# Adding up a selective scan's outputs with fp32 transposes in PSUM instead of identity products

## The chip, the cores and the metric

The kernel runs on one core of a Trainium2 chip. The metric is device time in microseconds (us) of one execution of the whole program. The engines are named as in the profile: PE (TensorE, matrix products; PEld are its weight loads), DVE (VectorE), ACT (ScalarE), POOL (GpSimd) and SP, which issues the DMA transfers.

## The reference, cut to what matters

The network has four layers on an image batch of shape 4 x 64 x 64 x 96. Layers 0 and 1 are state-space blocks ("block 0" and "block 1" here); layers 2 and 3 are attention and feed-forward layers on the pixels. Nearly all of the time goes to the two state-space blocks. Each of them scans its feature map in four directions: along rows, along columns, and both of these backwards. Block 1 works on the 64 x 33 half spectrum of the image.

```python
def step(hst, inputs):                       # one position l
    ul, dl, bl, cl = inputs
    dA = jnp.exp(dl[..., None] * A)          # A: channels x 16 states
    hst = hst * dA + (dl * ul)[..., None] * bl[:, :, None, :]
    y = jnp.einsum('bkdn,bkn->bkd', hst, cl) # sum over the 16 states of h * C
    return (hst, y)
...
ys = ys + Dskip[None, :, :, None] * u
...                                          # _cross_merge: the four directions joined
ys = ys[:, 0:2] + ys[:, 2:4][..., ::-1]
y1 = jnp.swapaxes(ys[:, 1].reshape(b, d, w, h), 2, 3).reshape(b, d, h * w)
y = ys[:, 0] + y1
...
y = (y - mu) * jax.lax.rsqrt(var + LN_EPS) * out_norm_w + out_norm_b
y = y * jax.nn.silu(z)
return y @ out_proj_w.T
```

What matters below is the sum over the 16 states of `h * C`, and how the four directions' sums meet: two of them are in row order and two in column order.

## The kernel before

Channels lie on the 128 partitions in three groups (`c`), positions along the free dimension. A direction is cut into segments of at most 512 positions. For a segment the 16 states are done in four quarters `q` of four states; one step of the loop does one quarter of one channel group: states 4q and 4q+1 as `hx`, 4q+2 and 4q+3 as `hy`. Per step DVE runs four hardware scans along the positions, POOL makes `hcx = hx * C` and the input of `hy`, DVE makes `hcy = hy * C`, ACT makes the exponentials and the scaled inputs `bx`, and PE transposes `bx` and adds up `hcx` and `hcy` in a PSUM bank for each channel group.

Six phases follow one another: two of block 0 (two images at a time, 384 steps each) and four of block 1 (one image each, 240 steps). Beside each phase a generator of "side" work is run in small pieces, at a fixed rate per step: the projections and convolutions of what comes next, and the merge, norm, output projection and later layers of what is done. `RATES` has the pieces per step.

```python
RATES = [0.65, 1.2, 2.0, 1.85, 1.85, 1.75]
CFG0 = Cfg("l0", 2, 1, HH, 0, 6, [(0, 32), (32, 64)], [8] * 8, [512] * 8, 1e-5)
CFG1 = Cfg("l1", 1, 2, WF, 1, 12, [(0, WF)], [7, 7, 7, 6, 6], [448, 448, 448, 384, 384], 1e-5)
# the last lists: rows of a norm block, positions of a segment

def accumulate(st, hc, n0):                  # L549: sum over states
    z = st.z
    for j in range(2):
        nc.tensor.matmul(z.acc[st.c][:, : z.S], ident, hc[:, j, : z.S],
                         start=(n0 + j == 0 and not z.opened), stop=(n0 + j == NST - 1))

def open_segment(z, before):                 # cut
    ...
    z.opened = z.k != 1
    for c in range(C):
        if z.k == 0:                         # L569: the skip term, once for all directions
            nc.tensor.matmul(z.acc[c][:, : z.S], z.blk.skip[:, c, :], z.u[:, c, : z.S], start=True, stop=False)
        if z.k >= 2:                         # L573: go on from the forward direction's sum
            yv = sp.tile([P, SM], F32, name=f"yv_{z.nm}_{c}", tag="yv", bufs=2)
            nc.sync.dma_start(out=yv[:, : z.S], in_=z.ph.io["y"][z.k % 2][:, c, z.a : z.a + z.S])
            nc.tensor.matmul(z.acc[c][:, : z.S], ident, yv[:, : z.S], start=True, stop=False)

# the loop over steps, cut (hx, hy, hcx and hcy each have one buffer)
    scan(st, hx, 0, st.ax[:, 0], st.px[0], 4 * q)          # DVE
    front_y(st, 1)                                         # ACT exp
    scan(st, hx, 1, st.ax[:, 1], st.px[1], 4 * q + 1)      # DVE
    ...
    nxt.px, nxt.ay = [transposed(nxt, 0)], {}              # PE, L501: 128x128 transposes of bx
    front_x(nxt)                                           # ACT exp
    nc.gpsimd.tensor_tensor(hcx[:, :, :S], hx[:, :, :S], z.c[q][0][:, :, :S], ALU.mult)
    take(bgen, per - per // 2); slot(False)                # ACT bx; side work
    scan(st, st.hy, 0, ...)
    nxt.px.append(transposed(nxt, 1))
    scan(st, st.hy, 1, ...)
    ...
    accumulate(st, hcx, 4 * q)                             # PE
    slot(True)                                             # side work
    nc.vector.tensor_tensor(hcy[:, :, :S], st.hy[:, :, :S], z.c[q][1][:, :, :S], ALU.mult)
    front_b(nxt)                                           # POOL: du * B into hy of the next step
    accumulate(st, hcy, 4 * q + 2)                         # PE
    if q == NQ - 1:                                        # the segment's sum leaves PSUM
        nc.scalar.copy(y[:, :S], z.acc[c][:, :S])          # ACT, L650
        nc.sync.dma_start(out=z.ph.io["y"][z.k % 2][:, c, z.a : z.a + S], in_=y[:, :S])

# side work: merge, cut. The two orders meet; `yo` is read with swapped axes
    pm = E.psum(f"py_{nm}_{r}")
    nc.tensor.matmul(pm[:, : n * 64], self.ident, v, start=True, stop=False)            # L283
    nc.tensor.matmul(pm[:, : n * 64].rearrange("p (r w) -> p r w", w=64), self.ident,   # L284
                     yo[:, :, r - p0 : r - p0 + n].rearrange("p w r -> p r w"), start=False, stop=True)
    E.defer(lambda v=v, pm=pm, n=n: nc.scalar.copy(v, pm[:, : n * 64]))
    ...                                                    # then to DRAM as `ym`; gated() reads `ym` and `gz`
```

Of the kernel before, what the change touches and what calls it, by code (L numbers as in the profile page):

```python
# [6 lines left out]
F32 = mybir.dt.float32  # L7
# [10 lines left out]
NB, HH, WW, CH = 4, 64, 64, 96  # L18
LTOK = HH * WW
WF = WW // 2 + 1  # L20
NST = 16
C, P = 3, 128
SM = 512
LATE = "late"

RATES = [0.65, 1.2, 2.0, 1.85, 1.85, 1.75]
# [22 lines left out]
CFG1 = Cfg("l1", 1, 2, WF, 1, 12, [(0, WF)], [7, 7, 7, 6, 6], [448, 448, 448, 384, 384], 1e-5)  # L49
# [44 lines left out]
class Block:  # L94
# [165 lines left out]
    def merge(self, E, g, ys, out):  # L260

        nc, cfg = self.nc, self.cfg
        ym = self.dram_tile("ym", (P, C, cfg.L), g)
        out["ym"] = ym
        PR = max(b - a for a, b in cfg.parts)
        with E.pool(f"{cfg.pre}mg{g}") as sp:
            for c in range(C):
                for p0, p1 in cfg.parts:
                    nm, pr = f"{cfg.pre}_{g}_{c}_{p0}", p1 - p0
                    yn = sp.tile([P, PR * 64], F32, name=f"yn_{nm}", tag="yn", bufs=2)  # L270
                    nc.sync.dma_start(out=yn[:, : pr * 64], in_=ys[cfg.nat][:, c, p0 * 64 : p1 * 64])
                    yo = sp.tile([P, 64, PR], F32, name=f"yo_{nm}", tag="yo", bufs=2)
                    nc.sync.dma_start(
                        out=yo[:, :, :pr],
                        in_=ys[1 - cfg.nat][:, c, :].rearrange("p (w r) -> p w r", r=cfg.NR)[:, :, p0:p1],
                    )
                    yield
                    for r, n in cfg.rows:
                        if not p0 <= r < p1:
                            continue  # L280
                        pm = E.psum(f"py_{nm}_{r}")
                        v = yn[:, (r - p0) * 64 : (r - p0 + n) * 64]
                        nc.tensor.matmul(pm[:, : n * 64], self.ident, v, start=True, stop=False)  # L283
                        nc.tensor.matmul(  # L284
                            pm[:, : n * 64].rearrange("p (r w) -> p r w", w=64),
                            self.ident,
                            yo[:, :, r - p0 : r - p0 + n].rearrange("p w r -> p r w"),
                            start=False,
                            stop=True,
                        )  # L290
                        E.defer(lambda v=v, pm=pm, n=n: nc.scalar.copy(v, pm[:, : n * 64]))
                        yield
                    nc.sync.dma_start(out=ym[:, c, p0 * 64 : p1 * 64], in_=yn[:, : pr * 64])
            yield

    def gated(self, E, g, ym, gz, out_proj):


        nc, cfg = self.nc, self.cfg
        with E.pool(f"{cfg.pre}nm{g}") as sp:  # L300
# [3 lines left out]
            def load(r, n):  # L304
                y = sp.tile([P, C, 512], F32, name=f"yb_{cfg.pre}_{g}_{r}", tag="yb", bufs=2)
                z = sp.tile([P, C, 512], F32, name=f"zb_{cfg.pre}_{g}_{r}", tag="zb", bufs=2)
                nc.sync.dma_start(out=y[:, :, : n * 64], in_=ym[:, :, r * 64 : (r + n) * 64])
                nc.sync.dma_start(out=z[:, :, : n * 64], in_=gz[:, :, r * 64 : (r + n) * 64])
                return y, z

            nxt = load(*cfg.rows[0])
            yield
            for b, (r, nr) in enumerate(cfg.rows):
                n = nr * 64
                nm = f"{cfg.pre}_{g}_{r}"
                y, z = nxt
                nxt = load(*cfg.rows[b + 1]) if b + 1 < len(cfg.rows) else None
# [62 lines left out]
def scans(tc, ctx, phases, ident):  # L380

# [164 lines left out]
    def accumulate(st, hc, n0):  # L546
        z = st.z
        for j in range(2):
            nc.tensor.matmul(  # L549
                z.acc[st.c][:, : z.S],  # L550
                ident,
                hc[:, j, : z.S],
                start=(n0 + j == 0 and not z.opened),
                stop=(n0 + j == NST - 1),
            )

    def open_segment(z, before):

        if z.first:
            z.state = [  # L560
                sp.tile([P, NST], F32, name=f"state_{z.nm}_{c}", tag=f"state{c}", bufs=2) for c in range(C)
            ]
        else:
            z.state = before.state
        z.acc = [ps.tile([P, 512], F32, name=f"acc_{z.nm}_{c}", tag=f"acc{c}") for c in range(C)]
        z.opened = z.k != 1
        for c in range(C):
            if z.k == 0:
                nc.tensor.matmul(z.acc[c][:, : z.S], z.blk.skip[:, c, :], z.u[:, c, : z.S], start=True, stop=False)  # L569
            if z.k >= 2:  # L570
                yv = sp.tile([P, SM], F32, name=f"yv_{z.nm}_{c}", tag="yv", bufs=2)
                nc.sync.dma_start(out=yv[:, : z.S], in_=z.ph.io["y"][z.k % 2][:, c, z.a : z.a + z.S])
                nc.tensor.matmul(z.acc[c][:, : z.S], ident, yv[:, : z.S], start=True, stop=False)  # L573
# [629 lines left out]
```

## Time and profile before

| | before |
|---|---|
| time, median of 3 runs | 14555.34 us (14533.06 to 14558.75) |
| span of the profiled execution | 14556.2 us |
| instructions | 140535 |
| mean granted PE clock | 0.919 |
| DMA | 1195619 packets, 1488.38 MB, mean 102 GB/s |
| POOL, products `du*B` and `hx*C` (L524, L630) | 3699.9 and 3716.2 us busy |
| DVE, product `hcy` (L644) | 1993.5 us busy |

The page gives each engine's busy time over the span. A group's line has the source line, engine, operation and tiles (`out<-in`), the shapes, the count, then the busy time and the mean duration of one, then the idle time of the engine just before such instructions and what ended it. A line of waits has who waited for whom, the total, how often, and the longest. In a timeline the first two numbers are start and duration. PE's matmuls overlap, so a group's busy time is less than count times mean. Where no row of the profile has a number asked for (the distance between two starts, the steps of a phase), it is counted from the starts and ends of the instructions in the same trace, and from its record of the granted clock.

### The profile page before, as it was taken

What the parts mean: (1) busy time and instruction counts of PE and PEld (TensorE: products, weight loads), DVE (VectorE), ACT (ScalarE), POOL (GpSimd) and SP (SyncE); (2) the same over time, 40 slices, a digit from 0 to 9 for tenths busy, and PEclk for the clock granted to TensorE, in tenths of its full rate; (3) what the DMA queues carried; (4) which work ended last, traced back from release to release, by engine and by line L of the source; (5) the groups of instructions that cost most, each with busy time, mean ns of one, the idle gap of its engine ahead of it and who ended that gap; (6) DMA issues with size and microseconds to landing.
All of it is one profiled execution on the core that took longest, in us unless ns stands there. A gap on an engine that the chain in (4) does not pass through costs nothing. (4 is left out here: it accounts for less than half of the span.)

```text
span 14556.2 us, 140535 instructions
## 1 busy us (share of the span) xinstructions
PE 12208.7 (84%) x42312; PEld 6312.6 (43%) x42312; DVE 10543.2 (72%) x10170; ACT 9388.2 (64%) x20401; POOL 7523.1 (52%) x3644
## 2 busy tenths in 40 slices
PE   5788888888888889889898888887888878888876
PEld 1344344434444444434544444444444444444434
DVE  0598788777886777786655676788767887678753
ACT  1577777776766667775555665676656666567643
POOL 0466666655655555564444454455544555445530
PEclk8899999999999999999998999899998999989885
DMA  4344444445443344435333333222332223322221
GB/s 116 106 115 116 111 115 112 111 113 133 123 107 108 108 101 111 127 98 145 103 107 99 119 114 90 86 78 93 114 88 86 79 91 114 90 88 76 78 98 27
DMA packets 1195619, 1488.38 MB, mean 102 GB/s; under 512 B 587043, under 2 KB 977903, under 8 KB 1178471
## 3 DMA queue, kind: packets, MB, share of 16 engines
q1 hardware_dynamic: 1194855, 1479.39, 35.5%
q8 instruction: 333, 5.46, 0.2%
q14 instruction: 431, 3.53, 0.1%
HBM read 1217.05 MB, written 262.06 MB: 102 GB/s over the span
## 5 line engine op out<-in xcount | busy, mean ns | idle before, releaser
L524 POOL TENSOR_TENSOR hy_l<-du_l,bc_l 128x1024 f32<-128x1024 f32 (+2 forms) x1728 | 3699.9, 2141 | 4770.6 <-DVE hcy_l L644 3063.7
L630 POOL TENSOR_TENSOR hcx_l<-hx_l,bc_l 128x1024 f32<-128x1024 f32 (+2 forms) x1728 | 3716.2, 2151 | 1271.0 <-PE acc_l L549 1074.3
L549 PE MATMUL acc_l<-hcy_l,ident 128*128 128x512 f32 (+2 forms) x6912 | 3177.1, 584 | 384.6 <-DVE hcy_l L644 381.9
L549 PE MATMUL acc_l<-hcx_l,ident 128*128 128x512 f32 (+2 forms) x6912 | 3326.6, 607 | 117.6 <-POOL hcx_l L630 114.4
L481 ACT ACTIVATE bx_l<-dut_l,bt_l 128x192 f32<-128x192 f32 (+2 forms) x6400 | 2847.5, 499 | 0.0
L644 DVE TENSOR_TENSOR hcy_l<-hy_l,bc_l 128x1024 f32<-128x1024 f32 (+2 forms) x1728 | 1993.5, 1154 | 596.7 <-PE acc_l L549 494.2
L506 ACT ACTIVATE ax_l<-delta_l,l_alog 128x512 f32<-128x512 f32 (+2 forms) x3456 | 2152.5, 670 | 75.2 <-DVE hx_l L529 75.1
L549 PEld LDWEIGHTS acc_l<-hcy_l,ident 128*128 128x128 f32 x6912 | 1315.2, 199 | 1949.6 <-issue 1048.5
L529 DVE TENSOR_TENSOR_SCAN hy_l<-ab_l,state_l,hy_l 128x448 f32<-128x448 f32 (+1 forms) x1512 | 1743.0, 1186 | 418.5 <-ACT ab_l L506 305.5
L529 DVE TENSOR_TENSOR_SCAN hx_l<-ax_l,state_l,ab_l 128x448 f32<-128x448 f32 (+1 forms) x1512 | 1735.8, 1182 | 327.7 <-PE ab_l L501 303.2
L529 DVE TENSOR_TENSOR_SCAN hy_l<-b_l,state_l,hy_l 128x512 f32<-128x512 f32 (+1 forms) x1368 | 1542.1, 1158 | 474.0 <-ACT b_l L506 370.5
L529 DVE TENSOR_TENSOR_SCAN hx_l<-ax_l,state_l,b_l 128x512 f32<-128x512 f32 (+1 forms) x1368 | 1538.0, 1155 | 320.9 <-PE b_l L501 290.9
L549 PEld LDWEIGHTS acc_l<-hcx_l,ident 128*128 128x128 f32 x6912 | 1275.4, 205 | 1011.7 <-issue 685.9
L506 ACT ACTIVATE ab_l<-delta_l,l_alog 128x448 f32<-128x448 f32 (+1 forms) x1824 | 1195.0, 655 | 708.6 <-DVE hx_l L529 677.2
L506 ACT ACTIVATE b_l<-delta_l,l_alog 128x512 f32<-128x512 f32 (+1 forms) x1632 | 1041.9, 638 | 721.7 <-DVE hx_l L529 665.2
L501 PE MATMUL ab_l<-ident,bx_l 128*128 128x128 f32 (+1 forms) x7296 | 1298.4, 288 | 218.1 <-DVE hy_l L529 123.0
L501 PEld LDWEIGHTS ab_l<-ident,bx_l 128*128 128x128 f32 (+1 forms) x7296 | 918.7, 145 | 1251.9 <-issue 633.3
L501 PE MATMUL b_l<-ident,bx_l 128*128 128x128 f32 x5760 | 988.3, 294 | 209.2 <-DVE hy_l L529 116.8
L650 ACT COPY y_l<-acc_l 128x512 f32<-128x512 f32 (+2 forms) x432 | 234.7, 543 | 1421.7 <-PE acc_l L549 1417.2
L501 PEld LDWEIGHTS b_l<-ident,bx_l 128*128 128x128 f32 x5760 | 728.1, 149 | 942.8 <-issue 375.2
L223 PE MATMUL pc_l<-pad_l,l_dg 128*128 128x512 f32 (+2 forms) x1944 | 854.4, 583 | 72.7 <-ACT uh_l L212 58.2
L542 ACT COPY state_l<-hx_l 128x2 f32<-128x2 f32 x1440 | 271.5, 189 | 540.5 <-DVE hx_l L529 538.3
(173 smaller groups left out, 10872.3 us busy)
## 6 DMA issues: line engine op xcount, KB each, us to landing
bc_l<-l_xd_l SPq DMA_DIRECT2D x1536, 256.0 KB
bc_l<-l_xd_l SPq DMA_DIRECT2D x576, 448.0 KB
bc_l<-l_xd_l SPq DMA_DIRECT2D x384, 384.0 KB
us_l<-l_u SPq DMA_DIRECT2D x64, 768.0 KB
l_y<-y_l SPq DMA_DIRECT2D x192, 256.0 KB
us_l<-l_u SPq DMA_DIRECT2D x48, 672.0 KB
l_y<-y_l SPq DMA_DIRECT2D x144, 224.0 KB
yv_l<-l_y SPq DMA_DIRECT2D x96, 256.0 KB
```

The lines of the kernel that those rows point to most:

```text
L223: nc.tensor.matmul(pc[:, : n * 64].rearrange("p (r w) -> p r w", w=64), diag[:, t, :], pad[:, r - p0 + dy : r - p0 + dy + n, dx : dx + 64] ...
L481: nc.scalar.activation(t[:n, b, :, ch], z.dut[:n, b, :, ch], AF.Copy, scale=z.bt[:n, b, m : m + 1])
L501: nc.tensor.transpose(pb[:, t : t + n], st.z.bx[st.q, j][:n, b, st.c], ident[:n, :n])
L506: nc.scalar.activation(out, z.delta[:, st.c, : z.S], AF.Exp, scale=z.blk.A[:, st.c, z.k, n : n + 1])
L524: nc.gpsimd.tensor_tensor(st.hy[:, :, :S], du, st.z.b[st.q][:, :, :S], ALU.mult)
L529: nc.vector.tensor_tensor_scan(h[:, j, : z.S][:, ::step], a[:, : z.S][:, ::step], b[:, : z.S][:, ::step], 0.0 if z.first else z.state[st.c ...
L542: nc.scalar.copy(z.state[st.c][:, n0 : n0 + 2].rearrange("p (j o) -> p j o", o=1), h[:, :, e : e + 1])
L549: nc.tensor.matmul(z.acc[st.c][:, : z.S], ident, hc[:, j, : z.S], start=(n0 + j == 0 and not z.opened), stop=(n0 + j == NST - 1),)
L630: nc.gpsimd.tensor_tensor(hcx[:, :, :S], hx[:, :, :S], z.c[q][0][:, :, :S], ALU.mult)
L644: nc.vector.tensor_tensor(hcy[:, :, :S], st.hy[:, :, :S], z.c[q][1][:, :, :S], ALU.mult)
L650: nc.scalar.copy(y[:, :S], z.acc[c][:, :S])
```

## The change

The sum over states is formed with the positions on the partitions. A product that has been made, `hc`, with channels on partitions, is the stationary operand of a 128 x 128 transpose, the identity is the moving one, and the transposes of all 16 states are added on top of one another in the PSUM bank; a segment of 512 positions takes four of them for each state. The sums go to DRAM as (direction forward or backward, position, channel). The skip term and the reload of the forward sums leave the scan, and so does the merge stage: the norm stage fetches the four sums of two rows of the map, and joins them by transposes back to channels on partitions, on top of the skip product. Row order and column order meet in the DRAM read, which takes a position's channels in one run. The segments and norm blocks of block 1 and the rates of side work are set anew.

```diff
-RATES = [0.65, 1.2, 2.0, 1.85, 1.85, 1.75]
+RATES = [0.65, 1.33, 2.15, 1.8, 1.8, 1.8]
-CFG1 = Cfg(... [7, 7, 7, 6, 6], [448, 448, 448, 384, 384], 1e-5)
+CFG1 = Cfg(... [8, 8, 6, 6, 5], [512, 512, 384, 384, 320], 1e-5)
 ... merge() removed; gated(), for two rows at a time:
+                yt = sp.tile([P, 2, 2, C * P], F32, name=f"yt_{nm}", tag="yt", bufs=2)
+                nc.sync.dma_start(
+                    out=yt[: n * 64, 0], in_=yn[:, r * 64 : (r + n) * 64, :].rearrange("k t c -> t k c")
+                )
+                for m in range(n):
+                    nc.sync.dma_start(out=yt[m * 64 : (m + 1) * 64, 1], in_=yo[r + m])
+                ut = sp.tile([P, C, P], F32, name=f"ut_{nm}", tag="ut", bufs=2)
+                nc.sync.dma_start(out=ut[:, :, : n * 64], in_=u[:, :, r * 64 : (r + n) * 64])
 ...
+                    for c in range(C):
+                        nc.tensor.matmul(
+                            ps[:, c, :m], self.skip[:, c, :], ut[:, c, :m], start=(c == 0), stop=False
+                        )
+                    yield
+                    for c in range(C):
+                        for k in range(4):
+                            nc.tensor.matmul(
+                                ps[:, c, :m],
+                                yt[:m, k // 2, k % 2, c * P : (c + 1) * P],
+                                self.ident[:m, :m],
+                                start=False,
+                                stop=(c == C - 1 and k == 3),
+                                is_transpose=True,
+                            )
+                        if c < C - 1:
+                            yield
+                    E.defer(lambda i=i, m=m, ps=ps, y=y: nc.scalar.copy(y[:, :, i * 64 : i * 64 + m], ps[:, :, :m]))
 ... accumulate():
-            nc.tensor.matmul(
-                z.acc[st.c][:, : z.S],
-                ident,
-                hc[:, j, : z.S],
-                start=(n0 + j == 0 and not z.opened),
-                stop=(n0 + j == NST - 1),
-            )
+            blocks = list(enumerate(z.blocks))
+            for b, (t, n) in blocks[:: 1 - 2 * j]:
+                nc.tensor.matmul(
+                    z.acc[st.c][:n, b, :],
+                    hc[:, j, t : t + n],
+                    ident,
+                    start=(n0 + j == 0 and b == 0),
+                    stop=(n0 + j == NST - 1 and b == 0),
+                    is_transpose=True,
+                )
 ... open_segment(): the skip product (L569) and the reload with its product (L573) removed
 ... at a segment's end:
+        y = sp.tile([P, NBK, P], F32, name=f"y_{st.nm}", tag="y", bufs=2)
+        for lo, hi, n in z.runs:
+            nc.scalar.copy(y[:n, lo:hi], z.acc[c][:n, lo:hi])
+            t = z.a + lo * P
+            nc.sync.dma_start(
+                out=z.ph.io["y"][z.k % 2][z.k // 2, t : t + (hi - lo) * n, c * P : (c + 1) * P].rearrange(
+                    "(b p) d -> p b d", p=n
+                ),
+                in_=y[:n, lo:hi],
+            )
```

## The prediction

> **What bounds the kernel now.** I read the page's first part, then busy time by stretch, then the groups by line, then the waits, then one step of the scan in the order of time. A step is one pass of the scan loop: two pairs of states of one 128-channel group of one segment. There are 1728 of them (768 in block 0 with S = 512, 960 in block 1 with S = 448 or 384). By the starts of the hcy products they fall into six phases, which begin at 533, 3406, 6568, 8588, 10398 and 12206 us; the scan ends at 14025. Each of the lines below is one stretch, with busy us of PE, PEld, DVE, ACT and POOL, then the granted clock.
>
> ```profile
> PE 12208.7 (84%) x42312; PEld 6312.6 (43%) x42312; DVE 10543.2 (72%) x10170; ACT 9388.2 (64%) x20401; POOL 7523.1 (52%) x3644
> ```
> ```profile
> 533.00:3406.00 2873.00, 2422.55 (x7840) 1161.63 (x7838) 2405.72 (x1992) 2168.02 (x4820) 1839.24 (x810) 0.95 0.41 112
> 3406.00:6568.00 3162.00, 2728.71 (x9193) 1407.30 (x9191) 2453.98 (x2042) 2223.98 (x4926) 1838.85 (x816) 0.94 0.42 114
> 6568.00:8588.00 2020.00, 1796.08 (x6273) 978.49 (x6273) 1319.91 (x1309) 1217.00 (x2474) 975.47 (x528) 0.93 0.38 113
> 8588.00:10398.00 1810.00, 1527.66 (x5656) 805.50 (x5656) 1394.40 (x1487) 1187.67 (x2583) 947.60 (x481) 0.93 0.29 92
> 14025.00:14556.00 531.00, 364.42 (x1398) 226.28 (x1396) 149.07 (x267) 139.26 (x335) 0.15 (x1) 0.61 0.19 52
> ```
>
> PE is the busiest engine in every phase, but DVE is close behind it in the first, and neither is full: the engines hand work round a ring, and PE is where it gets stuck. The groups by line and shape show what fills PE. A product in fp32 is recorded as two matmuls, so x3072 is 1536 products.
>
> ```profile
> L549 PE MATMUL acc_l<-hcx_l,ident 128*128 128x512 f32 x3072 | 1569.2, 636 | 73.5 <-POOL hcx_l L630 72.9
> L549 PE MATMUL acc_l<-hcy_l,ident 128*128 128x512 f32 x3072 | 1506.5, 614 | 105.6 <-DVE hcy_l L644 104.3
> ...
> L501 PE MATMUL ab_l<-ident,bx_l 128*128 128x128 f32 x6144 | 1059.9, 289 | 212.6 <-DVE hy_l L529 123.0 <-DVE hx_l L529 47.2 <-ACT bx_l L481 34.9
> ```
>
> The L549 products take 6503.7 us of PE in all (3326.6 + 3177.1), over half. The waits say what that costs:
>
> ```profile
> ACT y_l L650 <- PE acc_l L549: 1417.2, 415, 15.8
> POOL hcx_l L630 <- PE acc_l L549: 1074.3, 473, 11.4
> ...
> DVE hcy_l L644 <- PE acc_l L549: 494.2, 299, 8.9
> ...
> DVE hx_l L529 <- PE b_l L501: 394.3, 215, 6.3
> DVE hx_l L529 <- PE ab_l L501: 385.3, 177, 9.9
> ```
>
> ACT stands at a segment's end until the sums are whole, POOL and DVE cannot refill hcx and hcy until PE has read them, and the next scan's input comes late. Last, a step with little beside it (timeline, start and us first):
>
> ```profile
> 1007.76 1.22 DVE L644 TENSOR_TENSOR hcy_l<-hy_l,bc_l 128x1024 f32<-128x1024 f32 x1
> ...
> 1009.12 2.35 POOL L524 TENSOR_TENSOR hy_l<-du_l,bc_l 128x1024 f32<-128x1024 f32 x1 [1.81 <-ACT ab_l L506]
> 1009.18 1.88 PE L549 MATMUL acc_l<-hcy_l,ident 128*128 128x512 f32 x4
> ...
> 1011.39 0.66 PE L501 MATMUL ab_l<-ident,bx_l 128*128 128x128 f32 x4 [0.33 <-DVE hx_l L529]
> ...
> 1011.51 2.46 DVE L529 TENSOR_TENSOR_SCAN hy_l<-ab_l,state_l,hy_l 128x512 f32<-128x512 f32 x2 [0.17 <-POOL hy_l L524]
> ...
> 1014.07 1.23 DVE L644 TENSOR_TENSOR hcy_l<-hy_l,bc_l 128x1024 f32<-128x1024 f32 x1
> ```
>
> From hcy to hcy is 6.31 us here, and it is closed by DVE and POOL alone: hcy, the POOL product into the single hy buffer, two scans, hcy. That is the floor in block 0 (a tenth of phase 0's steps take 6.29 us or less), and the change leaves it alone. Phase 0 averages 7.48 us a step.
>
> **What the Trainium skill says.** "TensorE: Matmul & The Clock Gate", Terms, has transposes of fp32 through the array four times as fast as products; the trace shows a factor of two for the same columns: starts of successive L501 transposes lie 109 ns apart at full clock (213 at half), against 429 ns for each 512-wide half product, 107 ns per 128 columns of a half, two halves each. The same page, Part 4, holds that transposes do not count as activity for the clock. Here they do: among 3.4 us windows at full clock whose ordinary matmuls stream for 15 to 30% of the time, the next window is at half clock after all of those with under 10% of transposes and after 16% of those with 20 to 30%. "PSUM — Partial Sum Buffer", The four PSUM rules, says that a first matmul clears the flags of the whole bank and that an fp32 transpose sets them, so one start flag on block 0 suffices and transposes can add up; no run here shows their speed when they do.
>
> **The change, part by part.**
> Sums over states. A pair of L0 products costs 3075.7 / 1536 = 2.00 us of busy PE, in block 1 3427.9 / 1920 = 1.79. In their place stand 8 transposes per pair: 7 x 0.109 + 0.273 (the duration of one) = 1.04 us at full clock; with 8.5% of them at half clock and small gaps, 1.16. In block 1 the segments become 512, 512, 384, 384, 320, which are 17 blocks of positions instead of 18, so 6.8 transposes a pair, 1.00 us. Saved per step: 2 x 0.84 = 1.68 us and 2 x 0.79 = 1.57 us. Over 1536 and 1920 pairs PE falls from 6504 to about 3700, by 2800.
> Skip and reload in the scan (L569, L573). Gone: 94.3 + 239.6 us of PE, 0.19 per step, with 201.4 us in which PE waited for the reload.
> Merge stage. Gone: 113.0 + 190.0 us of PE (L283, L284), 58.1 of ACT, and the write and read of the merged tensor.
> Norm stage. Added: 2 x 32 + 4 x 17 = 132 tiles, each 3 skip products of 128 columns (6 halves of 0.107 + 0.164 of latency = 0.81) and 12 transposes (11 x 0.109 + 0.273 = 1.47): 301 us of PE, and a copy of 128x384 from PSUM, 444 ns by the group that copies dut, 59 us of ACT. It cancels the merge on both engines.
> PE in sum: 12208.7 - 2800 - 334 - 303 + 301 = about 9070. DVE is unchanged, and ACT nearly (128 fewer bx pieces).
> Side work: the rates rise because the side tasks have more pieces (461 against 364, 377 against 329). They are still used up before a phase ends, so no phase is left with a lump at its end.
>
> What this is worth is read from stretches of six steps, sorted by PE busy per step, with what a step takes beyond its DVE work. Phase 0 (DVE 6.27): PE 5.38 goes with 0.40 us beyond DVE, 6.33 (the mean) with 1.2, 7.20 with 1.91. Phase 2: 5.27 with 1.03, 7.23 with 2.56, 9.17 with 4.24. Phase 3: 4.66 with 0.80, 5.53 with 1.04, 7.47 with 2.57. I move each phase down its own curve by the saving, allowing for its spread:
> - Phase 0: PE 6.33 - 1.87 = 4.46, 0.35 beyond DVE, 6.62 a step, x 384 = 2540.
> - Phase 1 (DVE 6.40): 7.13 - 1.87 = 5.26, 0.75, 7.15, x 384 = 2745.
> - Phase 2 (DVE 5.50): 7.55 - 1.76 = 5.8, 1.4, 6.9, x 240 = 1655.
> - Phases 3 to 5 (DVE 5.82): 6.40 - 1.76 = 4.65, 0.8, 6.62, x 240 = 1590 each, 4770.
> - The start, 533, has none of the change. The end loses the merge, some 62 us from 14028 to the first norm matmul at 14090, and gains 17 small tiles that wait on loads only one tile ahead; at an estimated 4 to 5 us each that is as much. 545.
> Sum 12788; I say 12780. DVE's idle time within the scan, 13492 - 10354 = 3138 us, falls to about 1360.
>
> **Rivals.**
> A colder array. PE streams less, and windows that stream less than about 0.4 of their time are followed by half clock. The last stretch has PE 69% busy at a clock of 0.61. Against it: in the scan the transposes and side products still stream for over half of a step, and a cold window slows the work that fills it. I expect 0.85 instead of 0.92; 0.75 would add a quarter to 9070 us of PE, and the phases would slide back up their curves to about 13300.
> ACT takes PE's place. In phase 0 it is busy 5.66 us per step, 85% of 6.62, and it works in bursts: softplus between two table loads is 1.28 + 1.36 + 1.28 us in one piece. DVE's waits for ACT at hy, 439 + 379 us, need not shrink. If they double, about 13500; against it, part of them is ACT's own 1417 us behind PE.
> Adding transposes run at half the rate. 25344 x 0.104 us gives back 2640, and the time stays near 14400. Nothing in the trace speaks for it, nothing excludes it.
> Loads. Sums written positions first go out in pieces of 512 bytes, and each norm tile has four loads. The DMA engines are busy for 0.42 of the fullest phase, so I give this at most 100 us.
> DVE alone binds, with 0.1 us lost per step: 533 + 545 + 10354 + 170 = 11600. The curves never get there.
>
> **Range and chances.** The central sum rests on curves that end near the new loads; the clock and ACT are worth +500 each, fuller use of DVE -400. 12350 to 13300 should hold it 8 times in 10. Faster by over 2% means below 14264, which only the half-rate rival threatens: 0.95, 0.03, 0.02.
>
> **What would show it.** PE busy near 9100 to 9500 and no longer first by much; the L501 and sum transposes at 109 ns; ACT's wait for acc and POOL's wait for acc down by more than half; DVE over 80% of its span, hy waiting on POOL more often; the clock at 0.80 to 0.90. If sum transposes lie 200 ns apart at full clock, or the clock is below 0.75, or ACT holds hy for over 1500 us, the step that fails is the corresponding one.

## The result, and the profile after

| | before | after |
|---|---|---|
| time, median of 4 runs each | 14544.2 us (14524.21 to 14558.75) | 13887.4 us (13864.05 to 13924.31) |
| ratio, 95% interval | | 0.9552 (0.9527 to 0.9577) |
| span of the profiled execution | 14556.2 us | 13862.2 us |
| mean granted PE clock | 0.919 | 0.819 |
| PE busy | 12208.7 us | 10275.3 us |
| scan, first to last hcy product | 13492 us | 12791 us |

The change saves 657 us. The prediction was 1764, so the direction is right and the size is not: the time lies 1107 us above the 12780 predicted.

The page's first part and its row of granted clock, after (clock in tenths of full speed, one digit for each fortieth of the span):

```profile
PE 10275.3 (74%) x54680; PEld 7494.9 (54%) x54680; DVE 10488.4 (76%) x10170; ACT 9323.2 (67%) x20213; POOL 7524.9 (54%) x3644
...
PEclk8788888888888888988887888777887778877785
```

PE is now just below DVE, and no engine is near full. The same stretches as before, by the new starts of the phases (phases 0 to 3, then the end; columns as in the prediction):

```profile
527.00:3275.00 2748.00, 1973.32 (x10773) 1430.02 (x10772) 2398.17 (x1994) 2172.95 (x4824) 1838.90 (x811) 0.86 0.42 113
3275.00:6222.00 2947.00, 2211.03 (x12596) 1708.90 (x12594) 2440.42 (x2040) 2225.74 (x4928) 1837.56 (x816) 0.87 0.45 120
6222.00:8101.00 1879.00, 1512.84 (x7893) 1102.18 (x7894) 1315.20 (x1310) 1194.37 (x2430) 978.86 (x529) 0.83 0.42 121
8101.00:9846.00 1745.00, 1311.44 (x7044) 970.51 (x7044) 1384.17 (x1486) 1171.84 (x2531) 947.78 (x481) 0.78 0.31 93
13318.00:13862.00 544.00, 370.41 (x1652) 254.17 (x1651) 149.66 (x267) 139.47 (x336) 0.15 (x1) 0.62 0.23 57
```

Phase 0 went from 2873 to 2748 us while PE's busy time in it fell by 449; phase 3 from 1810 to 1745 while PE fell by 216. Nothing moved at the start (533 and 527) or at the end (531 and 544). The groups of the sums and of the new norm stage:

```profile
L554 PE MATMUL acc_l<-ident,hcx_l 128*128 128x128 f32 (+1 forms) x12132 | 2048.1, 322 | 160.7 <-POOL hcx_l L645 155.7
L554 PE MATMUL acc_l<-ident,hcy_l 128*128 128x128 f32 (+1 forms) x12126 | 1942.1, 310 | 575.3 <-DVE hcy_l L659 573.3
...
L308 PE MATMUL py_l<-ident,yt_l 128*128 128x128 f32 (+1 forms) x1584 | 253.3, 290 | 0.6 <-DMA yt_l<-l_y 0.6
...
L302 PE MATMUL py_l<-ut_l,l_skip 128*128 128x128 f32 (+1 forms) x792 | 143.3, 327 | 123.4 <-ACT yb_l L318 87.9 <-DMA ut_l<-l_u 28.2 <-ACT ab L754 5.8
```

With two smaller groups of the same line (216 us), L554 takes 4206 us in place of 6504. PE now waits longer for hcy (573 us, 382 before). The waits of the ring, after:

```profile
ACT y_l L581 <- PE acc_l L554: 1073.9, 393, 8.5
...
PE acc_l L554 <- DVE hcy_l L659: 573.3, 442, 8.1
...
DVE hx_l L532 <- PE b_l L504: 466.0, 262, 5.4
...
DVE hy_l L532 <- ACT b_l L509: 368.7, 190, 13.1
...
POOL hcx_l L645 <- PE acc_l L554: 339.8, 169, 10.8
...
DVE hy_l L532 <- POOL hy_l L527: 284.1, 1069, 4.8
...
DVE hy_l L532 <- ACT ab_l L509: 210.3, 97, 13.0
...
DVE hcy_l L659 <- PE acc_l L554: 177.4, 117, 9.2
```

Against the lines of before: POOL and DVE wait far less for PE to read hcx and hcy (1074 to 340, 494 to 177), as meant. But DVE's waits for PE at hx fell little (780 to 466 and a line of 185, 651 in sum), and those for ACT at hy by less than a third (818 to 579). Within the scan DVE stood idle for 3138 us before and 2492 after (12791 less the 10299 that it was busy); the prediction had it down to 1360.

A segment is twelve steps (three channel groups times four quarters). Sorted by place in the segment, from hcy to hcy, in us (the 1st is the time from a segment's first hcy to its second; lumps over 25 us left out):

```
phase 0      1st  2nd  3rd  4th  5th  6th  7th  8th  9th  10th 11th 12th  mean
before       8.15 7.08 6.90 9.81 8.12 6.29 6.64 6.89 6.62 7.31 7.59 8.41  7.48
after        6.60 7.07 6.44 9.90 8.06 6.30 6.64 7.04 6.52 6.89 6.96 7.45  7.16
phase 3
before       8.98 7.03 7.63 8.51 7.81 7.46 6.93 7.17 6.14 7.50 7.36 7.99  7.54
after        6.88 7.11 7.45 8.95 7.79 6.78 6.66 6.98 6.48 7.50 7.41 7.27  7.27
```

The gain is not spread over the steps, although the PE time that the transposes save is. The largest part lies in the first step of a segment (1.55 of 3.9 us a segment in phase 0, 2.1 of 3.3 in phase 3), much of the rest around its end; the fourth, which is the longest now, got no shorter.

### The profile page after: what moved, and what is told of

It reads as the page before. It is cut to its first block, busy times and chain, and to the rows that moved or that the text cites. A ratio compares the mean times of both kernels' runs of the same rounds, so it can differ in the third digit from the quotient of the medians.

```text
span 13862.2 us, 165415 instructions
## 1 busy us (share of the span) xinstructions
PE 10275.3 (74%) x54680; PEld 7494.9 (54%) x54680; DVE 10488.4 (76%) x10170; ACT 9323.2 (67%) x20213; POOL 7524.9 (54%) x3644
## 5 line engine op out<-in xcount | busy, mean ns | idle before, releaser
L554 PE MATMUL acc_l<-ident,hcy_l 128*128 128x128 f32 (+1 forms) x12126 | 1942.1, 310 | 575.3 <-DVE hcy_l L659 573.3
L532 DVE TENSOR_TENSOR_SCAN hy_l<-b_l,state_l,hy_l 128x512 f32<-128x512 f32 (+2 forms) x1696 | 1860.1, 1130 | 452.3 <-ACT b_l L509 311.5
L532 DVE TENSOR_TENSOR_SCAN hx_l<-ax_l,state_l,b_l 128x512 f32<-128x512 f32 (+2 forms) x1696 | 1864.4, 1128 | 414.6 <-PE b_l L504 388.4
L554 PE MATMUL acc_l<-ident,hcx_l 128*128 128x128 f32 (+1 forms) x12132 | 2048.1, 322 | 160.7 <-POOL hcx_l L645 155.7
L554 PEld LDWEIGHTS acc_l<-ident,hcy_l 128*128 128x128 f32 (+1 forms) x12126 | 1630.9, 161 | 967.3 <-DVE hcy_l L659 737.6
L554 PEld LDWEIGHTS acc_l<-ident,hcx_l 128*128 128x128 f32 (+1 forms) x12132 | 1704.3, 167 | 322.8 <-POOL hcx_l L645 302.9
L509 ACT ACTIVATE b_l<-delta_l,l_alog 128x512 f32<-128x512 f32 (+2 forms) x1960 | 1227.9, 627 | 649.1 <-DVE hx_l L532 616.2
L532 DVE TENSOR_TENSOR_SCAN hy_l<-ab_l,state_l,hy_l 128x512 f32<-128x512 f32 x981 | 1211.5, 1270 | 264.9 <-ACT ab_l L509 172.8
L504 PE MATMUL ab_l<-ident,bx_l 128*128 128x128 f32 x5272 | 989.8, 318 | 485.3 <-DVE hx_l L532 302.6
L532 DVE TENSOR_TENSOR_SCAN hx_l<-ax_l,state_l,ab_l 128x512 f32<-128x512 f32 x982 | 1209.5, 1266 | 137.4 <-PE ab_l L504 129.1
```

What stands on the lines that cost most here:

```text
L504: nc.tensor.transpose(pb[:, t : t + n], st.z.bx[st.q, j][:n, b, st.c], ident[:n, :n])
L509: nc.scalar.activation(out, z.delta[:, st.c, : z.S], AF.Exp, scale=z.blk.A[:, st.c, z.k, n : n + 1])
L532: nc.vector.tensor_tensor_scan(h[:, j, : z.S][:, ::step], a[:, : z.S][:, ::step], b[:, : z.S][:, ::step], 0.0 if z.first else z.state[st.c ...
L554: nc.tensor.matmul(z.acc[st.c][:n, b, :], hc[:, j, t : t + n], ident, start=(n0 + j == 0 and b == 0), stop=(n0 + j == NST - 1 and b == 0), ...
```

## The experiments

The theories, as they stood after this reading:

- *PE*: the prediction's own, that a us of PE busy is worth about half a us wherever it lies.
- *Side*: what a step takes above the ring's floor is what side work costs on the other engines and in the order of their programs; PE time saved is worth little against it.
- *Softplus*: the fourth step is one fixed burst of ACT, once a segment, which no change of PE touches.
- *Clock*: the colder array gave back what the transposes saved.
- *Opening*: what was gained is the skip product and the reload at a segment's first step, and not the cheaper sums.
- *Cuts*: the new segments and rates explain a part.

**1 and 2. Both kernels without side work beside the scan.** All of it is run between the phases, so nothing is left out of the computation.

```diff
-RATES = [0.65, 1.2, 2.0, 1.85, 1.85, 1.75]        # before; likewise in after
+RATES = [0.0] * 6
```

> Kernel before with all rates at 0: the side work is run in one lump at each phase's end, so the steps of the scan stand alone. Time is not compared, only the mean step (before: 7.48, 8.23, 8.42, 7.54, 7.54, 7.61 us in phases 0 to 5). Side theory (the curve of step time against PE busy time that the prediction used is mostly a curve against side work): the steps drop to 6.9 in block 0 and 6.1 in block 1, nearly as low as in the changed kernel without side work. PE theory (the sums on PE are what makes steps long): they stay above 7.2 and 6.6. Softplus theory (ACT's softplus between two table loads is the fixed part): the fourth and fifth step of a segment stay at 9 to 10 and 8 us in phase 0, as now (9.81 and 8.12).

> Changed kernel with all rates at 0. Mean step now 7.16, 7.68, 7.83, 7.27, 7.25, 7.24 us. Side theory: 6.7 in block 0 and 5.9 in block 1, within 0.3 us of the kernel before without side work. PE theory: 6.6 and 5.8, at least 0.6 us below it. Softplus theory: the fourth and fifth step of a segment still take 9 to 10 and 8 us in phase 0, all the others 6.3 to 6.6. Clock theory (half clock stretches the steps): with still less for PE to do the granted clock in the scan falls below 0.75, and steps do not get shorter than with side work.

Measured, in one execution of each: 6.90 us a step before and 6.66 after in block 0, 5.95 and 5.70 in block 1 (lumps between the phases not counted). A plain step takes 6.31 us in block 0 and 5.36 in block 1 in both kernels: this floor is the ring of DVE and POOL, and the change does not touch it. Nor does the clock, which was 0.97 in these steps before and 0.85 after (the clock theory had it below 0.75). The first step takes 8.35 us before and 6.31 after in phase 0 (7.4 to 8.0 and 5.36 in block 1), the second and, in block 0, the twelfth are a little shorter too; the fourth takes 8.88 and 9.07. So with all PE time to spare the change is worth 0.24 us a step, and that sits where segments open and close.

The scan alone adds up to 768 x 6.90 + 960 x 5.95 = 11011 us before and 768 x 6.66 + 960 x 5.70 = 10587 after. Side work therefore costs some 2480 us before (13492 less 11011) and 2200 after. The side theory stands: the prediction had given the scan with side work 6.62 us a step in phase 0, less than the changed kernel takes there with none.

**3. Softplus without table loads (after).** The Trainium skill, "ScalarE: Activation LUTs", section "Table sets: the hidden batching unit", has exp and ln in one set. The page puts a switch of sets at about 2.7 us, half of it the load and half a drain; here the load takes 1.28 us too, but no drain is to be seen, and softplus starts 0.02 us behind it. The timeline of a fourth step of the changed kernel:

```profile
1380.18 1.28 ACT L432 ACT_TABLE_LOAD   x1
...
1381.48 1.48 ACT L432 ACTIVATE delta_l<-delta_l 128x1536 f32<-128x1536 f32 x1
...
1382.98 1.28 ACT L433 ACT_TABLE_LOAD   x1
...
1384.28 0.69 ACT L509 ACTIVATE ab_l<-delta_l,l_alog 128x512 f32<-128x512 f32 x1
...
1385.00 1.28 DVE L532 TENSOR_TENSOR_SCAN hy_l<-ab_l,state_l,hy_l 128x512 f32<-128x512 f32 x1 [2.15 <-ACT ab_l L509]
```

For 4.1 us ACT makes no exponential for the scan, and DVE stands 2.15 us at the second hy scan. The edit makes softplus as ln(1 + exp(x)) of each channel group:

```diff
-            nc.scalar.activation(z.delta[:, c, :S], pd[:, :S], AF.Identity, bias=...)
-        nc.scalar.activation(z.delta[:, :, :S], z.delta[:, :, :S], AF.Softplus)
-        nc.scalar.preload_act_table_set(EXP_LN)
+            nc.scalar.activation(z.delta[:, c, :S], pd[:, :S], AF.Exp, bias=...)
+            nc.scalar.activation(z.delta[:, c, :S], z.delta[:, c, :S], AF.Ln, bias=blk.one)
```

> Changed kernel with softplus made of Exp and Ln, one channel group at a time, which needs no table loads: ACT's piece of some 4 us (1.28 + 1.48 + 1.28) is gone, the two Identity and softplus passes become Exp and Ln. Softplus theory: the fourth and fifth steps fall from 9.9 and 8.06 us to about 6.7, some 4 us a segment or more, 144 segments: 500 to 650 us less, about 13300. Clock theory: PE's cold stretches are what is left, under 150 us less. Side theory: 150 to 300 us less, since those steps then meet other side work.

Measured: 13631.5 us (ratio 0.9369, 0.9353 to 0.9384), 256 below the changed kernel. The fourth step fell from 8.9 to 7.3 us in phases 3 to 5 and from 10.25 to 8.1 in phase 1, but only from 9.9 to 9.4 in phase 0. The fifth kept its 8.1 us in phase 0 (it holds DVE's product for du). The softplus theory had put 500 to 650 us on this edit; the gain lies where the side theory had it.

**4. Warming the array (after).** A product with a zero weight tile, which adds nothing to the sums, after the hcx transposes of every step: 1318 us of streaming at full clock (0.858 us in block 0, 0.686 in block 1), to keep the clock up.

```diff
             accumulate(st, hcx, 4 * q)
+            nc.tensor.matmul(z.acc[c][:, :full, :], zero, hcx[:, 0, : full * P]..., start=False, stop=False)
```

> Changed kernel with one more product per step, a zero matrix times hcx added to the same sums (it adds nothing): 858 ns of streaming on PE at full clock, 1728 times, 1480 us at most. It keeps the array warmer. Clock theory: the granted clock rises from 0.82 to 0.90 and more, and the time falls by 150 us or more in spite of the work. PE theory (PE time per step still sets the pace as in the prediction's curves, about 0.5 us per us): the time rises by 500 us or more. Softplus theory: PE has room in most steps, so the time moves by less than 200 us either way.

Measured: 14001.16 us (0.9623, 0.9606 to 0.964). The clock rose from 0.819 to 0.877, and the time by 114 us. PE's busy time rose by only 712 us, since the warmer array did its other work sooner. The clock theory falls, as far as warming by added work can test it.

**5. The kernel before without the opening.** The skip product and the reload of the forward sums with its load are taken out. This leaves out the skip term, and the forward sums do not enter the result.

```diff
-        z.opened = z.k != 1
+        z.opened = False
-            if z.k == 0:      # skip product
+            if False:
-            if z.k >= 2:      # reload and product
+            if False:
```

> Kernel before without the three products that open a segment's sums (skip or reload) and without the reload's loads; it leaves out the skip term and the forward sums. Without side work, the kernel before and the changed one differ by 0.24 us a step, and nearly all of that is in the first step of a segment (8.35 against 6.31 us in phase 0, 7.67 against 5.36 in phase 3). Opening theory (those products and loads are what the change took off the path): the first step falls to 6.5 to 7 us and the time by 300 to 450 us, to about 14150, more than half of the change's 660. PE theory (only the sums over states count): 334 us less of PE, at the prediction's 0.5 us per us at most 170 us, about 14400.

**6. The changed kernel with an opening put back.** In the 1st, 3rd and 4th direction a segment opens with a load of its inputs and a product of them with zero for each group.

```diff
+        if z.k != 1:
+            for c in range(C):
+                nc.sync.dma_start(out=yv[:, : z.S], in_=z.ph.io["u"][z.k % 2][:, c, z.a : z.a + z.S])
+                nc.tensor.matmul(z.acc[c][:, :f, :], zero, yv[:, : f * P]..., start=True, stop=False)
```

> Changed kernel with three products put back at the opening of a segment of the first, third and fourth direction, with a load each, as before: a zero matrix times a loaded piece of the scan's input, which adds nothing. Opening theory: the first step of a segment rises by about 1 to 2 us on average and the time by 250 to 400 us, to about 14200. PE theory: under 120 us more.

Measured: taking it out of before gives 14255.45 us (0.9796, 0.9782 to 0.9811; 14553.32 for the kernel before timed beside it), putting it into after 14181.15 (0.9746, 0.9732 to 0.9761): 298 us less and 294 more. The first step goes from 8.15 to 6.82 us in phase 0 of before, and from 6.60 to 8.85 in phase 0 of after. From both sides, opening is worth nearly 300 us, close to half of the gain.

PE's busy time moved by 283 and 278 us, as if a us of PE cost a whole us here; but the directions point to the load and not to the products. In the kernel before, the first direction opens with the skip product alone, whose inputs are on the chip; the third and fourth open with a load and its product, the second with nothing. Without side work (run 1, phase 0) their first steps take 6.31, 10.51, 10.27 and 6.31 us, in this order: the skip product costs nothing there, the reload about 4 us. And of what run 5 saved, 270 us lie in the two directions that reload, 24 in the first, and 13 in the second, which the edit does not touch. One opening of the kernel before shows why:

```profile
1385.51 1.79 PE L573 MATMUL acc_l<-yv_l,ident 128*128 128x512 f32 x2 [3.09 <-DMA yv_l<-l_y]
...
1387.09 1.91 PE L501 MATMUL ab_l<-ident,bx_l 128*128 128x128 f32 x8
...
1388.29 2.45 DVE L529 TENSOR_TENSOR_SCAN hx_l<-ax_l,state_l,ab_l 128x512 f32<-128x512 f32 x2 [3.33 <-PE ab_l L501]
```

PE stands 3.09 us for the load, the transposes of the next step's input stand behind it in PE's program, and DVE waits 3.33 us for them. Run 6 gives the first direction a load too, and that direction then takes 121 us more; so the closeness of 298 and 294 is in part chance. No run took out the load and kept the product.

**7. Cuts alone (before).** The new segments, norm rows and rates in the kernel before.

```diff
-RATES = [0.65, 1.2, 2.0, 1.85, 1.85, 1.75]
+RATES = [0.65, 1.33, 2.15, 1.8, 1.8, 1.8]
-CFG1 = Cfg(... [7, 7, 7, 6, 6], [448, 448, 448, 384, 384], 1e-5)
+CFG1 = Cfg(... [8, 8, 6, 6, 5], [512, 512, 384, 384, 320], 1e-5)
```

> Kernel before with the changed kernel's segments of block 1 (512, 512, 384, 384, 320) and rates of side work, nothing else. Cuts theory (new cuts and rates bring part of the gain): 100 us or more below the kernel before. All other theories: within 100 us of it, since DVE's work is the same and there is one block of 128 positions in 18 less to scale and transpose.

Measured: 14599.22 us (1.0034, 1.0023 to 1.0045), 46 us slower than the kernel before timed beside it. The cuts theory falls.

**8. Giving back the PE time of the transposes (after).** Two zero products a step, one after the hcx transposes, one ahead of the hcy transposes: some 2635 us of streaming, about what the transposes had saved.

```diff
+            nc.tensor.matmul(z.acc[c][:, :full, :], zero, hcx[:, 0, : full * P]..., start=False, stop=False)
 ...
+            nc.tensor.matmul(z.acc[c][:, :full, :], zero, hcy[:, 0, : full * P]..., start=False, stop=False)
             accumulate(st, hcy, 4 * q + 2)
```

> Changed kernel with two zero products per step, one before each half of the sums' end: nearly all of the PE time that the transposes saved in the scan is spent again (2 x 858 ns of streaming of some 1690 ns saved per step in block 0). With one the time rose by 114 us and the clock to 0.877. Side theory (the transposes' saving lies beside DVE and POOL nearly everywhere): 250 to 400 us above the changed kernel, about 14200, with the clock above 0.9. PE theory, the prediction's curves: 1000 us or more above it. Clock theory: below the run with one.

Measured: 14315.02 us (0.9838, 0.9821 to 0.9854), 428 above the changed kernel (the side theory had 250 to 400, the PE theory 1000 or more), at a clock of 0.915, nearly that of before. So 2635 us of streaming are worth 0.16 us each; per us of PE busy, which rose by 1571, it is 0.27. The parts nearly add up: 298 for the opening, 428 for the sums with their clock, less 46 for the cuts, are 680 us, against 657 measured. What the exchange of the merge for the new norm stage is worth by itself was not run.

**9. Warming where PE stands idle (after).** Two zero products of 256 columns behind the transposes of bx, in nine of twelve steps, 1110 us of streaming.

```diff
                 nxt.px, nxt.ay = [transposed(nxt, 0)], {}
+                warm(st, hx)          # 256 columns against zero, where st.q > 0
```

> Changed kernel with two half-size zero products (256 columns, 429 ns of streaming each) in nine of twelve steps, set where PE stands waiting for DVE in a plain step, right after each group of transposes of the next step's input. Streaming: 1728 x 0.75 x 2 x 429 ns = 1110 us, but beside other work. Clock theory (the array falling to half clock is what ate the gain): clock 0.87 or more, time 100 us or more below the changed kernel's 13887. PE theory: 150 us or more above it, as every us of PE counts. If both hold in part, within 80 us of it.

Measured: 14126.42 us (0.9707, 0.9692 to 0.9721), 239 us slower at a clock of 0.881, on the side of the PE theory (150 or more). Even there PE is not free: 0.22 us of time per us of streaming, 0.42 per us of PE busy, which rose by 572. A run that warms the array and costs PE nothing was not found, so what half clock costs by itself stays open.

**10. Softplus without table loads, and no side work (after).** The edits of 3 and 2 together.

```diff
-RATES = [0.65, 1.33, 2.15, 1.8, 1.8, 1.8]         # from the kernel of experiment 3
+RATES = [0.0] * 6
```

> Softplus from Exp and Ln, side work in lumps at the phases' ends; only the mean step counts (changed kernel without side work: 6.66 in block 0, 5.71 in block 1; its fourth step 9.07 and 8.2). Softplus theory: the fourth step falls to 6.5 to 7 and 5.5 to 6, the fifth stays (7.77 and 6.6: it holds DVE's du product), the mean becomes 6.45 and 5.5. Otherwise the fourth step stays above 8 and 7, and something else than the table loads makes it long (the single PSUM bank that hands three groups in turn from PE to ACT).

Measured: the fourth step takes 6.87 us in phase 1 (9.07 with the loads) and 5.9 to 6.2 in block 1 (8.2). In phase 0 it takes 12.56. The groups of table loads of this kernel say why:

```profile
L434 ACT ACT_TABLE_LOAD x96 | 123.2, 1283 | 1.7
...
L510 ACT ACT_TABLE_LOAD x94 | 120.6, 1283 | 1.7
```

All of them lie in phase 0: there each Ln loads one table and the next Exp another, until a set with both is resident. Outside phase 0 the softplus theory is confirmed.

**11. The same softplus in the kernel before.**

```diff
-        nc.scalar.activation(z.delta[:, :, :S], z.delta[:, :, :S], AF.Softplus)    # as in 3
+            nc.scalar.activation(z.delta[:, c, :S], z.delta[:, c, :S], AF.Ln, bias=blk.one)
```

> Kernel before with softplus from Exp and Ln. Separate-causes theory: the softplus step is as long before as after, so the gain is the same as in the changed kernel, 200 to 310 us. If softplus became the bound only by the change, the gain here is under 120 us.

Measured: 14355.94 us (0.9864, 0.985 to 0.9879), 204 below the kernel before timed beside it. Softplus costs both kernels nearly the same, so it explains what the change could not reach, and not where an expected gain went.

**12. No side work in the two steps that make delta** (on the kernel of 3; the rate is raised by a little over 12/10 elsewhere).

```diff
+            if (st.q, st.c) not in ((1, 0), (1, 1)):
                 due += st.z.ph.rate / 2
```

> Changed kernel with softplus from Exp and Ln, and no side work in the two steps of a segment in which delta is made; the rates are raised by 12/10 so that the side work still fits. Collision theory (side pieces that meet the delta chain on PE and ACT are worse than elsewhere): 80 us or more below soft_after's 13632. Otherwise within 60 us of it, since side work costs the same wherever it is.

Measured: 13805.38 us (0.9486, 0.947 to 0.9502), 174 slower. Those two steps did get shorter (8.0 to 5.8 us in phase 2, the fourth), and the others more than lost it. That side work collides only with delta is wrong: it costs wherever it stands.

**13. The table loaded in phase 0** (on 3): the first segment alone keeps the old softplus, which is followed by the load of the set with both.

```diff
+            if z is segs[0]:  # Identity here, Softplus and the preload behind the loop, as before
+            else:             # Exp, Ln
```

> soft_after, but the first segment keeps softplus, so that the table with Exp and Ln is loaded in the first phase too (in soft_after the fourth step of phase 0 took 12.5 to 13.2 us in its first ten segments, with a table load at each Exp and Ln). Softplus theory: those ten fall to about 7 us, 55 to 70 us in all, to about 13565; phases 1 to 5 as in soft_after.

Measured: 13553.02 us (0.9313, 0.9298 to 0.9329), 78 below 3; the fourth step of phase 0 fell from 9.4 to 7.53 us.

**14. Order: half a step more for side results** (on 13). A new theory, *order*: DVE runs its program in order, and a side instruction on it that needs a result of PE or ACT holds up the scan behind it. The timeline of one 11.34 us step of the changed kernel:

```profile
8288.50 1.48 PE L429 MATMUL pp_l<-xs_l,l_dtw 44*128 44x384 f32 x2 [1.28 <-ACT delta_l L431]
...
8289.92 2.08 PE L322 MATMUL pm_l<-yb_l,l_mean_w 128*128 128x512 f32 x2
...
8292.03 1.88 DVE L326 TENSOR_TENSOR yb_l<-yb_l,pm_l 128x512 f32<-128x512 f32 x3 [4.49 <-PE pm_l L322]
...
8293.83 0.95 DVE L659 TENSOR_TENSOR hcy_l<-hy_l,bc_l 128x768 f32<-128x768 f32 x1
...
8294.93 1.81 POOL L527 TENSOR_TENSOR hy_l<-du_l,bc_l 128x768 f32<-128x768 f32 x1 [7.15 <-DVE hcy_l L659]
```

The second hy scan ended at 8287.54, so hcy could have run then. It stands behind a subtraction of the norm stage, which waits 4.49 us for its means; PE makes those late because it in turn stood behind delta. POOL, which refills hy, waits 7.15 us. The edit puts a further yield, half a step, between the producer and such DVE instructions (mean subtraction, residual sums, attention and feed-forward); the rates rise with the pieces.

```diff
+                yield
                 for c in range(C):          # subtraction of the mean, L326
 ...
             yield
+            yield
             nc.vector.tensor_tensor(xr, xr, po, ALU.add)      # four more of this kind
-RATES = [0.65, 1.33, 2.15, 1.8, 1.8, 1.8]
+RATES = [0.65, 1.42, 2.28, 2.08, 2.08, 2.08]
```

> soft2 with half a step more between the PE or ACT result and the side instruction that uses it, for the mean's subtraction, the residual sums, and the two feed-forward adds and relu; rates raised to fit. In the changed kernel DVE stands idle some 540 us straight ahead of side instructions. Order theory: 150 us or more below soft2. PE-time theory: within 60 us of it.

Measured: 13350.57 us (0.9174, 0.916 to 0.9187), 202 below 13. DVE's waits at side instructions, in the kernel of 13 first, then here:

```profile
DVE y L1021 <- ACT y L1019: 104.5, 55, 4.4
DVE tok L984 <- PE pao L982: 95.5, 49, 3.7
...
DVE h L1003 <- ACT h L1000: 74.3, 64, 2.5
```
```profile
DVE tok L988 <- PE pao L985: 36.4, 21, 4.4
...
DVE y L1027 <- ACT y L1024: 30.5, 21, 2.5
...
DVE h L1008 <- ACT h L1004: 23.2, 25, 1.9
```

The three fell from 274 to 90 us. In all, DVE's idle time straight ahead of side instructions within the scan was 565 us before, 544 after the change, 498 in 13 and 194 here; ahead of the scan's own instructions it did not fall (1664 and 1777). The order theory holds (it had 150 us or more), though the new yields also spread out the side work of PE and ACT, which was not run apart. This kernel is the fastest of the study: 537 us below the changed one.

**15. Less PE work on the side (after).** Three of the nine taps of the convolution; six are left out.

```diff
-                                start=(t == 0), stop=(t == 8),
+                            if t < 3:       # around the product
+                                start=(t == 0), stop=(t == 2),
```

> Changed kernel with three of the nine taps of the convolution; it leaves out the other six. 108 row blocks x 6 x 858 ns = 556 us less of side products on PE at full clock, most of it in phases 0 to 2 and some before the scan (18 to 24 of the 108 blocks lie in the start stage, where PE is the path: 110 us). PE-time theory: 300 us or more less in phases 0 to 2, as a PE us in a burst counts for most of itself. Order theory: under 150 us less there, and the rest of side work's cost stays.

Measured: 13657.38 us (0.9385, 0.9371 to 0.9399), 230 below the changed kernel. Of this 118 lie at the start, where no scan runs; phases 0 to 2 give 108 us, while the taps' busy time in them fell by 396 us (from 681 to 285): 0.27 per us, as in 8. The order theory had under 150 us there, the PE theory 300 or more. The rest of those phases' excess stayed, so most of it is not the amount of PE work on the side.

## Why the prediction was wrong in size

**The failed step** is the one that turns PE time into time: "I move each phase down its own curve by the saving." It made 3139 us of PE (12208.7 to 9070) worth 1764, or 0.56 each. The curve was a correlation, and the trace of before shows with what. Of phase 0's stretches of six steps, the quarter with the least PE time has 5.21 us a step of the scan's own work on PE and 0.23 of side work; the quarter with the most has 4.99 and 2.31. In phase 3 it is 4.27 and 0.54 against 5.05 and 3.20. So what moves along the curve is mostly side work, which lengthens a step through DVE, ACT and the order of the programs as well as through PE; the sums, which the change makes cheaper, hardly do. Moving down the curve took side work away along with the PE time. Runs 1 and 2 show it for phase 0 (6.66 us with no side work, 6.62 predicted with it). Nor does the curve hold at the PE time that was really reached: the prediction reads 0.40 us beyond DVE at 5.38 us of PE in phase 0, and 1.04 at 5.53 in phase 3; the changed kernel has less PE time, 5.14 and 5.46 (1973.32 / 384, 1311.44 / 240), and more beyond DVE, 0.91 and 1.50. Runs 4, 8, 9 and 15 show what a us of busy PE in the middle of a step was traded for: 0.16, 0.27, 0.42 and 0.27 us (114 / 712, 428 / 1571, 239 / 572, 108 / 396), not 0.56.

**PE's sum.** 9070 was predicted and 10275 measured. The sums fell to 4206, not to about 3700: the prediction had 8.5% of the transposes at half clock, and it was 29% (6383 of 21888, by the distances below). The rest of PE's work is 6069 us where 5370 was expected, at a clock of 0.82 where 0.85 was expected. The norm stage took 397 us (143.3 + 253.3) instead of 301. So PE's time fell by 1933 us and not by 3139: this second step was right in kind and failed by its size. At the predicted 0.56 the 1206 us would make about 680 of the missing 1107 us; read from the curves, which flatten towards low PE time, they make less. How the miss divides is not shown: no run gave PE its warm clock back without giving it work as well.

**Skip and reload.** They were put at 0.19 us of PE a step and thrown in with the rest. They were the best part, 298 us of time, and nearly all of it lies in the directions that reload: as far as these tell it, not for the product but for the wait at its load, ahead of the next step's transposes (run 6; first step 8.35 against 6.31 us in runs 1 and 2). The prediction named this wait, 201.4 us, and gave it no time of its own. So close to half of the gain came by a way that it had not counted on.

**The sum transposes.** Right: the median distance of their starts is 109 ns at full clock (15505 of them) and 213 at half (6383), so the rival of half rate is dead.

**ACT in PE's place.** The waits at hy did not double; they fell to 579 us. But the softplus burst that this rival named was real: with its loads gone (3 and 13) the changed kernel gains 334 us. It cost both kernels nearly the same (204 us before, in 11, and 256 after, in 3).

**A colder array.** The clock came out at 0.819, within 0.80 to 0.90. Warming by added work (4, 8, 9) made every kernel slower.

**Loads, start and end.** 527 and 544 us against 533 and 545 predicted: right. The chain of new norm tiles costs the end what the merge had cost.

**The signs that were named.** POOL's wait for acc fell by more than half, ACT's did not (1417 to 1074); hy waited on POOL a little more often (1069 times, 1019 before); DVE came to 76% and not over 80%, PE to 10275 us and not to 9500 at most.

**What stays open.** The fastest kernel's scan takes 12262 us, and without side work the kernel of 10 needs 768 x 6.49 + 960 x 5.54 = 10303 (phase 1's mean taken for both phases of block 0). Of the 1960 us between them DVE's side work is 617 and its idle time ahead of that 194. Where the other 1150 arise, in ACT's or PE's order, was not separated. Nor was the cost of half clock alone.

## What to carry to other kernels

A busy engine's saving is worth what its place in a step makes it: run the main loop without its side work, and put the saved time back as work that adds nothing, before trusting a curve of step time against busy time. Look at the places where loops open and where in-order engines must wait for somebody else's result: a reload that PE waited for lengthened its step by about 4 us, while a us of busy PE in the middle of a step was worth 0.16 to 0.42. Give a side instruction on the bounding engine half a step of slack behind its producer.

## What the runs showed of the hardware

Transposes of fp32 that add up in one PSUM bank run at the pace of plain ones, 109 ns apart. They also count for the clock, against the Trainium skill's "TensorE: Matmul & The Clock Gate", Part 4. Summed up over each window of 3.4 us at full clock, with 107 ns for every 128 columns of a recorded matmul, the streaming after the change reads so: where products fill under 15% of a window and transposes under 30%, half clock follows in 99% of cases (371 windows); where products fill as little and transposes over 40%, in 0.5% (609). In both traces nearly every window with less than 0.35 of streaming in all is followed by half clock (264 of 265 before, 515 of 515 after), and 1 to 2% of those above 0.5. The clock fell so 363 times before and 648 after: here a saving on the array made the array slower, 0.819 of its clock in place of 0.919. And ACT loads a table at nearly every change between Exp and Ln in the first phase of experiment 10 (190 loads, 1.28 us each), and at none once the set with both had been loaded in that phase (13).
